# Statistics of the second image in layer 0: pieces of 512 pixels instead of 256, at six places of a period, loaded by ScalarE's queue

## The chip, the cores and the metric

The kernel runs on one core of a Trainium2 chip. The metric is the device time of one execution in microseconds; lower is better. Before the change it is 3701.71 us, the median of three runs (3700.44 to 3704.26). The engines are named as in the profile: PE is TensorE (PEld its weight loads), DVE is VectorE, ACT is ScalarE, POOL is GpSimd, SP is the engine that here only issues transfers.

## What is computed

Two images of 512 channels and 64 x 64 pixels go through two residual layers. Each layer first normalizes its input over groups of 16 channels and all pixels of an image. That is why an image's statistics must be complete before any of its pixels can be normalized.

```python
def _gn(v, G=32, eps=1e-5):
    g = v.reshape(B_, G, C_ // G, H_, W_)
    m = mean(g, axis=(2, 3, 4)); s = var(g, axis=(2, 3, 4))
    return ((g - m) / sqrt(s + eps)).reshape(v.shape)

x = x + _L0_conv_ref(_gn(x), ...)   # deformable convolution: project, depthwise 3x3,
                                    # layer norm over channels, gelu, offsets and masks,
                                    # bilinear samples summed over 9 points, output matrix
x = x + _L1_conv_ref(_gn(x), ...)   # attention over all pixels, matrix, batch norm, relu
```

The change touches only how `mean` and `var` of `_gn(x)` in layer 0 are gathered for the second image.

## The kernel before

**Tiling.** Channels lie on the 128 partitions in four blocks (`KB = 4`), pixels along the free axis in chunks of 512 (`CH`), which are eight rows of an image (`NCH = 8` chunks an image, 16 in all, `NSEQ`). All data are fp32.

**Stages of layer 0 for a chunk.** Each stage is a Python generator, and each `yield` ends a step:
- `project(i)` loads rows (`raw`, L737), normalizes them on ACT (`xn`, L748), multiplies them with `in_w` on PE (`pq`, L758), copies the result on ACT (`xj`, L764) and has SP store it to memory (`xt`, L766).
- `features(i)` is the depthwise convolution: one tap a channel block on ACT (L783), the other eight on DVE (`conv`, L788), then sums over channels: POOL adds the blocks (`tot`, L794 and L796), PE sums over partitions with a matrix of ones (`p_mean`, L801), DVE subtracts (L806), ACT squares (L809), POOL and PE sum again, ACT takes the root (L818), DVE the reciprocal (L820) and the product (L821), ACT the gelu (L825).
- `weights(i)` computes offsets and masks with PE (`po`, L842), adds a bias on DVE (`o`, L847) and makes sampling weights in a chain of pairs on DVE (`pk`, L885, and `aw`, L890); ACT copies them (`at`, L893), PE transposes them (`p_tr`, L901), ACT copies the result (`awT`, L902).
- `sample(i)` spreads the weights with PE (`pb`, L930) and ACT (`bt`, L935), multiplies with patches that SP has fetched from `xt` (`patch`, L914, eight transfers of 192 KB a fetch, two fetches a chunk) into `pa` (L949), which ACT copies to `dT` (L960); then the output matrix (`py`, L969), a residual add on DVE (L974) with statistics for layer 1 (L975), and SP stores the result (`wx`, L976).

**The period.** The 16 chunks are worked through in 16 periods. The function `period(y, v, m, w, f, g, p, more)` is an order written out by hand. It advances generators of several chunks by given numbers of steps: in period i, `p` is `project(i+3)`, `f` is `features(i+2)`, `w` is `weights(i+1)`, `v` the rest of `weights(i)` (its transposes), `m` is `sample(i)` and `y` the rest of `sample(i-1)`. Inside `tc.manual_schedule()` each engine executes its instructions in the order in which the program issues them, and waits for others by semaphores. A transfer is also issued in this order on the queue of the engine that is told to issue it, and holds that queue until what it waits for is done.

**The statistics.** `image_stats(n)` is one more generator. For image 0 it reads tiles that are in SBUF already, before the periods start. For image 1 it is the tail `later`, advanced by `more()`. Each step takes one piece of one channel block from memory (`xraw`, L711, three buffers, so loads run up to three pieces ahead) and has DVE make its statistics (`bn_stats`, L713). After the last piece of a block DVE combines them (`bn_aggr`, L715). Then `group_norm_steps` sums over the 16 channels of a group with two small matmuls (L602, L611), takes the root on ACT (L615) and the reciprocal on DVE (L618). Whatever is left of `later` is run in one go before period 5:

```python
for i in range(NSEQ):
    if i == NCH - 3:
        run(later)
    w, m, g = Chain(weights, i + 1), Chain(sample, i), Chain(features, i + 3)
    period(y, v, m, w, f, g, Chain(project, i + 3), lambda: next(later, None))
    y, v, f = m, w, g
```

Before the change a piece has 256 pixels, so image 1 has 4 x 16 = 64 of them; `period` calls `more()` at 13 places, eight in the loop over `taps` (two a round) and five in its second half; and SP issues the loads.

Of the kernel before, what the change touches and what calls it, by code (L numbers as in the profile page):

```python
# [9 lines left out]
F32 = mybir.dt.float32  # L10
# [7 lines left out]
P = 128  # L18
NB = 2
C = 512  # L20
KB = C // P
H = W = 64
S = H * W
# [7 lines left out]
CH = 512  # L31
NCH = S // CH
# [538 lines left out]
def window_path(ctx: ExitStack, tc: tile.TileContext, t_in: dict, out: bass.AP, far: bass.AP, sums: bass.AP):  # L571
    nc = tc.nc
    x_v = t_in["x"].rearrange("n (cb p) h w -> n p cb (h w)", p=P)
# [25 lines left out]
    def group_norm_steps(mv, k, small, psum, result):  # L599

        p1 = psum.tile([P, CH], F32, tag="mm", name="gn_p1")
        nc.tensor.matmul(p1[:, : 2 * k], gmat, mv.rearrange("p k s -> p (k s)"), start=True, stop=True)  # L602
        yield
        gm = small.tile([P, k, 2], F32, name=f"gn_gm{k}")
        nc.vector.tensor_copy(gm.rearrange("p k s -> p (k s)"), p1[:, : 2 * k])
        d = small.tile([P, k], F32, name=f"gn_d{k}")
        nc.vector.tensor_sub(d, mv[:, :, 0], gm[:, :, 0])
        nc.vector.tensor_mul(d, d, d)
        yield
        p2 = psum.tile([P, CH], F32, tag="mm", name="gn_p2")  # L610
        nc.tensor.matmul(p2[:, :k], gmat, d, start=True, stop=True)  # L611
        yield
        var = small.tile([P, k], F32, name=f"gn_var{k}")
        nc.vector.tensor_add(var, gm[:, :, 1], p2[:, :k])
        nc.scalar.activation(var, var, AF.Sqrt, bias=eps)  # L615
        yield
        sc = small.tile([P, k], F32, name=f"gn_sc{k}")
        nc.vector.reciprocal(sc, var)  # L618
        bi = small.tile([P, k], F32, name=f"gn_bi{k}")
        nc.vector.scalar_tensor_tensor(bi, gm[:, :, 0], -1.0, sc, ALU.mult, ALU.mult)  # L620
        result += [sc, bi]
# [8 lines left out]
    with ExitStack() as l0:  # L630
        wp = l0.enter_context(tc.tile_pool(name="w0w", bufs=1))
        io = l0.enter_context(tc.tile_pool(name="w0io", bufs=1))
        cv = l0.enter_context(tc.tile_pool(name="w0conv", bufs=1))
        sm = l0.enter_context(tc.tile_pool(name="w0small", bufs=1))
# [10 lines left out]
        img = [bt.rearrange("p g q d -> p (g q d)")[:, h * S : (h + 1) * S] for h in range(2)]  # L645
# [51 lines left out]
        def image_stats(n):  # L697

            mv = sm.tile([P, KB, 2], F32, name="gn_mv")
            size = CH if n == 0 else CH // 2  # L700
            pieces, ahead = deque((kb, h) for kb in range(KB) for h in range(S // size)), deque()
            for kb in range(KB):
                st = sm.tile([P, 16, 6], F32, name="gn_st")
                for h in range(S // size):
                    if n == 0:
                        t = img[kb][:, h * size : (h + 1) * size]
                    else:
                        while len(ahead) < 3 and pieces:
                            k2, h2 = pieces.popleft()
                            ahead.append(io.tile([P, size], F32, name="xraw", bufs=3))  # L710
                            nc.sync.dma_start(ahead[-1], x_v[n, :, k2, h2 * size : (h2 + 1) * size])  # L711
                        t = ahead.popleft()
                    nc.vector.bn_stats(st[:, h, :], t)  # L713
                    yield
                nc.vector.bn_aggr(mv[:, kb, :], st[:, : S // size].rearrange("p a b -> p (a b)"))  # L715
            yield
            result = []
            yield from group_norm_steps(mv, KB, sm, ps, result)
            sc, bi = result
            gn[n] = [sm.tile([P, KB], F32, name=f"gn_{k}{n}") for k in ("scale", "bias")]  # L720
            nc.vector.tensor_copy(gn[n][0], sc)
            nc.vector.tensor_copy(gn[n][1], bi)
# [275 lines left out]
        def period(y, v, m, w, f, g, p, more):  # L998

            p()
            y()
            v(4)
            f(4)
            y()
            for taps in (9, 7, 6, 6):
                m(2)
                w()  # L1010
                more()
                f(taps)
                w()
                more()
            w()
            m()
            w()
            m()
            f()
            y()  # L1020
            f()
            m()
            p()
            w(2)
            y(2)
            w()
            m()
            p()
            f()
            w(2)  # L1030
            p()
            y(2)
            f()
            y()
            m()
            p()
            more()
            for k, steps in enumerate((1, 2, 2, 2)):
                p()
                w(steps)  # L1040
                if k == 0:
                    f()
                p()
                more()
                if k < 3:
                    m()
                if k == 0:
                    f()
                if k == 2:
                    g()  # L1050
            w()
# [17 lines left out]
        def output_bias():  # L1069
# [8 lines left out]
            yield  # L1078

        run(image_stats(0), project(0), value_weights(), features(0), project(1))  # L1080
        v = Chain(weights, 0)
        v(23)
        run(features(1), project(2), output_bias())
        fetch(0, 0)
        fetch(0, 1)
        later, y, f = image_stats(1), Chain(sample, NSEQ), Chain(features, 2)
        with tc.manual_schedule():
# [7 lines that stand above are left out]
            y.rest()  # L1095
# [5 lines left out]
    with ExitStack() as l1, tc.manual_schedule():  # L1101
# [8 lines left out]
        with ExitStack() as at, ExitStack() as inner:  # L1110
# [69 lines left out]
            mv = bnp.tile([P, NB * KB, 2], F32, name="mv2")  # L1180
# [107 lines left out]
            for n in range(NB):  # L1288
# [9 lines left out]
                for i in range(NCH // 2):  # L1298
                    if 0 < i < 3 or n and i == 0:
                        k = i + 1 if i else 1  # L1300
# [26 lines left out]
                for qb in range(NCH):  # L1327
# [48 lines left out]
                    a = [acc[j].rearrange("p (cb q) -> p cb q", cb=2) for j in range(6)]  # L1376
# [156 lines left out]
```

## Time and profile before

The profiled execution took 3707.44 us; its span, from first to last instruction, is 3705.57 us.

| what | value |
|---|---|
| median of three runs | 3701.71 us |
| profiled execution, span | 3707.44 us, 3705.57 us |
| PE busy | 3417.9 us (92%) |
| DVE busy | 2345.8 us (63%) |
| ACT busy | 1304.1 us (35%) |
| mean granted TensorE clock | 0.968 |
| layer 0's periods 0 to 15 | about 172 to 1276 us |
| image 1's statistics, first to last | 175.1 to 533.0 us |

The page shows the span in 40 equal slices of 92.6 us. A digit is the busy share of the slice in tenths; in the row PEclk it is the granted clock in tenths.

```profile
PE   4689998999998799999999999999999999999990
DVE  5798989999996475545554554567455455545544
ACT  2476777787886321111111111221111111111114
PEclk9789999999999899999999999999999999999995
```

Layer 0 is the first third, where DVE, PE and ACT are all busy; layer 1 is the rest, where PE is. In the lists of instructions below, `out<-in` are names of tiles, then come partitions x elements and the count; brackets hold the idle time of the engine ahead of the instruction and what ended it. SPq and ACTq are the queues' own instructions, the issues of transfers.

### The profile page before, as it was taken

To read this page: it belongs to the slowest core of one execution; us is meant where nothing else is said; L and a number is where in the kernel's file an instruction comes from. 1 tells how busy PE (TensorE), PEld (TensorE's weight loads), DVE (VectorE), ACT (ScalarE), POOL (GpSimd) and SP (SyncE) were. 2 spreads that over 40 slices of the span, in tenths; PEclk is the share of its full clock that TensorE was granted. 3 is DMA by queue.
4 is the path that set the end of the run, shared out by engine and by line. 5 is a ranking of instruction groups with operands and counts; after the bars stand their busy time and mean duration, and the time that the engine had idled before them with its cause. 6 is when DMAs were issued, how large, how long until landed. Compare 5 with 4: busy or idle time off the path is not lost.

```text
span 3705.6 us, 39010 instructions
## 1 busy us (share of the span) xinstructions
PE 3417.9 (92%) x15151; PEld 2433.8 (66%) x15151; DVE 2345.8 (63%) x3575; ACT 1304.1 (35%) x1691; POOL 291.0 (8%) x190
## 2 busy tenths in 40 slices
PE   4689998999998799999999999999999999999990
PEld 1355555555555477777777777777777777777770
DVE  5798989999996475545554554567455455545544
ACT  2476777787886321111111111221111111111114
POOL 2112111212111030000000000022000000000000
PEclk9789999999999899999999999999999999999995
DMA  7233442342432444334334333444433333243349
GB/s 240 63 98 114 135 137 83 115 133 83 127 109 78 142 157 171 126 129 139 123 108 163 122 125 130 140 155 169 149 121 111 122 138 111 101 149 121 111 162 389
DMA packets 180181, 500.06 MB, mean 135 GB/s; under 512 B 22640, under 2 KB 64368, under 8 KB 170512
## 3 DMA queue, kind: packets, MB, share of 16 engines
q1 hardware_dynamic: 176496, 473.34, 37.5%
q10 hardware_dynamic: 3456, 24.12, 1.7%
q8 instruction: 121, 1.98, 0.2%
q14 instruction: 76, 0.62, 0.0%
q0 software_dynamic: 32, 0.00, 0.0%
HBM read 406.09 MB, written 91.29 MB: 134 GB/s over the span
## 4 chain that ended last, share of the span: by engine, by line
PE 75%; DVE 15%; DMA 4%; ACT 2%; SPq 1%; issue 1%; POOL 1%; ACTq 0%; DVEq 0%; POOLq 0%
PE acc L1364 41%; DVE conv L788 8%; PE pS L1211 7%; PE p L1402 7%; PE py L969 5%; PE pq L758 4%; PE pa L949 4%; PE pv L1251 3%; PE pk L1305 1%; PE p_mean L801 1%; DVE pk L885 1%; DVE aw L890 1%; DMA patch<-xt 1%; DMA out<-ct 1%; DVE o L847 1%
## 5 line engine op out<-in xcount | busy, mean ns | idle before, releaser
L1364 PE MATMUL acc<-e,v 128*128 128x256 f32 x3072 | 768.2, 386 | 0.0
L1215 ACT ACTIVATE e<-pS 128x1024 f32<-128x1024 f32 x256 | 262.0, 1024 | 1386.4 <-PE pS L1211 1313.0
L1364 PE MATMUL acc<-tt,v 128*128 128x256 f32 x3072 | 748.2, 380 | 0.5 <-DMA v<-wv 0.5
L1364 PEld LDWEIGHTS acc<-e,v 128*128 128x128 f32 x3072 | 566.5, 190 | 233.2 <-issue 165.3
L1364 PEld LDWEIGHTS acc<-tt,v 128*128 128x128 f32 x3072 | 582.4, 190 | 91.2 <-issue 10.6
L1218 DVE TENSOR_TENSOR t<-e 128x256 f32<-128x256 f32 x256 | 108.8, 425 | 761.1 <-ACT e L1215 761.1
L788 DVE SCALAR_TENSOR_TENSOR conv<-xn,L_conv_dw_w_sb,conv 128x504 f32<-128x504 f32 (+1 forms) x512 | 399.7, 795 | 48.5 <-ACT conv L783 36.5
L1228 DVE TENSOR_TENSOR tot<-tot,e 128x512 f32<-128x512 f32 x480 | 330.1, 688 | 8.3
L949 PEld LDWEIGHTS pa<-bt,patch 96*128 96x128 f32 x2048 | 251.8, 197 | 63.1 <-issue 39.4
L1211 PE MATMUL pS<-q,kq 64*128 64x512 f32 x1024 | 289.0, 641 | 0.0
L949 PE MATMUL pa<-bt,patch 96*128 96x128 f32 x2048 | 255.3, 281 | 9.3 <-ACT dT L960 5.8
L935 ACT COPY bt<-pb 96x1024 f32<-96x1024 f32 x124 | 234.2, 2001 | 58.9 <-PE pb L930 58.9
L758 PE MATMUL pq<-L_conv_in_w_sb,xn 128*128 128x512 f32 x512 | 236.3, 605 | 4.3 <-ACT xn L748 4.3
L969 PE MATMUL py<-dT,L_conv_out_w_sb 128*128 128x512 f32 x512 | 238.0, 610 | 0.0
L1402 PE MATMUL p<-t,v 128*128 128x256 f32 x1024 | 231.4, 382 | 1.7 <-DMA v<-wv 1.7
L1402 PEld LDWEIGHTS p<-t,v 128*128 128x128 f32 x1024 | 192.1, 190 | 48.5 <-issue 21.2
L960 ACT COPY dT<-pa 32x256 f32<-32x256 f32 x496 | 179.5, 362 | 89.8 <-PE pa L949 80.9
L842 PE MATMUL po<-om_w_pg,feat 128*128 128x432 f32 x512 | 203.4, 542 | 0.0
L969 PEld LDWEIGHTS py<-dT,L_conv_out_w_sb 128*128 128x128 f32 x512 | 99.3, 197 | 119.6 <-issue 115.5
L758 PEld LDWEIGHTS pq<-L_conv_in_w_sb,xn 128*128 128x128 f32 x512 | 94.1, 194 | 109.5 <-issue 93.0
L842 PEld LDWEIGHTS po<-om_w_pg,feat 128*128 128x128 f32 x512 | 93.0, 191 | 90.5 <-issue 89.4
L1211 PEld LDWEIGHTS pS<-q,kq 64*128 64x128 f32 x1024 | 77.1, 184 | 84.9 <-issue 84.9
(203 smaller groups left out, 3731.2 us busy)
## 6 DMA issues: line engine op xcount, KB each, us to landing
v<-wv SPq DMA_DIRECT2D x252, 768.0 KB
patch<-xt SPq DMA_DIRECT2D x256, 192.0 KB
v<-wv SPq DMA_DIRECT2D x256, 128.0 KB
wv<-v SPq DMA_DIRECT2D x32, 896.0 KB
xt<-xj SPq DMA_DIRECT2D x128, 128.0 KB
res<-in_x SPq DMA_DIRECT2D x64, 256.0 KB
wx<-res SPq DMA_DIRECT2D x64, 256.0 KB
xq<-wx SPq DMA_DIRECT2D x16, 1024.0 KB
```

Source lines behind the costliest of these rows:

```text
L758: nc.tensor.matmul(pq, xn[:, kb, 1 + 2 * t : 3 + 2 * t, :].rearrange("p r c -> p (r c)"), in_w[:, kb, :], start=(kb == 0), stop=(kb == KB ...
L788: nc.vector.scalar_tensor_tensor(dst, src, wt, dst, ALU.mult, ALU.add)
L842: nc.tensor.matmul(po[:, : 3 * GP], f[:, kb, t * P : (t + 1) * P], om_w[:, kb].rearrange("p a k g -> p (a k g)"), start=(kb == 0), stop=(k ...
L935: copy(bt[:SN].rearrange("s g q d -> s d (g q)")[:, d0 : d0 + 4, :], pb[:SN])
L949: nc.tensor.matmul(pa[:, p], xp[:SN, p, cb * P : (cb + 1) * P], bt[:SN, 4 * cb : 4 * cb + 4, PX * s + p, :], start=True, stop=True,)
L960: copy(dst, src)
L969: nc.tensor.matmul(py, out_w[:, kb, cb * P : (cb + 1) * P], dT[:, kb, :], start=(kb == 0), stop=(kb == KB - 1))
L1211: nc.tensor.matmul(pS[:, h, :], kq[r, 2 * (kp // 4) + h, c0 : c0 + P], qs[qb][r, :], start=True, stop=True)
L1215: nc.scalar.activation(e.rearrange("p a q -> p (a q)"), pS.rearrange("p h q -> p (h q)"), AF.Exp)
L1228: nc.vector.tensor_add(tots[qb], tots[qb], e2[:, h, :])
L1364: nc.tensor.matmul(acc[j][:, cb * HQ : (cb + 1) * HQ], v[:, j, cb * P : (cb + 1) * P], ops[j], start=(kp + cb == 0), stop=(kp + cb == NPAI ...
L1402: nc.tensor.matmul(p7[:, cb * HQ : (cb + 1) * HQ], v7[:, cb * P : (cb + 1) * P], t3, start=(k + cb == 0), stop=(k + cb == NPAIR + 2),)
```

## The change

A piece of image 1 now has 512 pixels, as one of image 0 has; there are 32. The buffers `xraw` double in size and stay three. The loads are issued by ACT's queue. `more()` is called at six places of a period instead of 13: after `v(4)`, after `f(4)`, in the rounds of 9 and 7 taps (after `f(taps)` and `w()`), in the second half after `y(2)` and before the step of `f` that holds the reciprocal, and once in the last loop (at `k == 2`).

```diff
             mv = sm.tile([P, KB, 2], F32, name="gn_mv")
-            size = CH if n == 0 else CH // 2
-            pieces, ahead = deque((kb, h) for kb in range(KB) for h in range(S // size)), deque()
+            pieces, ahead = deque((kb, h) for kb in range(KB) for h in range(NCH)), deque()
             for kb in range(KB):
-                st = sm.tile([P, 16, 6], F32, name="gn_st")
-                for h in range(S // size):
+                st = sm.tile([P, NCH, 6], F32, name="gn_st")
+                for h in range(NCH):
                     if n == 0:
-                        t = img[kb][:, h * size : (h + 1) * size]
+                        t = img[kb][:, h * CH : (h + 1) * CH]
                     else:
+
                         while len(ahead) < 3 and pieces:
                             k2, h2 = pieces.popleft()
-                            ahead.append(io.tile([P, size], F32, name="xraw", bufs=3))
-                            nc.sync.dma_start(ahead[-1], x_v[n, :, k2, h2 * size : (h2 + 1) * size])
+                            ahead.append(io.tile([P, CH], F32, name="xraw", bufs=3))
+                            nc.scalar.dma_start(ahead[-1], x_v[n, :, k2, h2 * CH : (h2 + 1) * CH])
                         t = ahead.popleft()
                     nc.vector.bn_stats(st[:, h, :], t)
                     yield
-                nc.vector.bn_aggr(mv[:, kb, :], st[:, : S // size].rearrange("p a b -> p (a b)"))
+                nc.vector.bn_aggr(mv[:, kb, :], st.rearrange("p a b -> p (a b)"))
```

```diff
             v(4)
+            more()
             f(4)
+            more()
             y()
             for taps in (9, 7, 6, 6):
                 m(2)
                 w()
-                more()
                 f(taps)
                 w()
-                more()
+                if taps in (7, 9):
+                    more()
...
             y(2)
+            more()
             f()
             y()
             m()
             p()
-            more()
             for k, steps in enumerate((1, 2, 2, 2)):
                 p()
                 w(steps)
                 if k == 0:
                     f()
                 p()
-                more()
+                if k == 2:
+                    more()
```

## The prediction

> **What bounds the kernel now.** I read the stretches first. I cut layer 0 where a period's first channel-mean matmul (`p_mean`, L801) starts, because that is where TensorE waits for VectorE. Columns: stretch, length, then busy time (instructions) of PE, PEld, DVE, ACT, POOL, then granted clock, DMA share, GB/s.
>
> ```profile
> core 0: us, PE busy (x) PEld busy (x) DVE busy (x) ACT busy (x) POOL busy (x), PEclk, DMA share, GB/s
> 203.20:275.00 71.80, 59.53 (x285) 37.73 (x285) 64.15 (x80) 53.84 (x74) 13.34 (x9) 0.88 0.38 119
> 275.00:351.70 76.70, 67.49 (x309) 39.27 (x309) 67.18 (x86) 53.76 (x72) 12.97 (x9) 0.95 0.40 122
> 351.70:426.00 74.30, 66.66 (x308) 39.06 (x308) 66.49 (x85) 53.69 (x73) 12.96 (x9) 0.96 0.40 126
> 426.00:500.00 74.00, 67.08 (x308) 39.21 (x308) 67.05 (x86) 53.77 (x73) 12.98 (x9) 0.96 0.39 125
> 500.00:575.30 75.30, 66.43 (x313) 39.52 (x313) 65.33 (x85) 55.07 (x75) 12.96 (x10) 0.95 0.33 103
> 575.30:646.00 70.70, 67.44 (x309) 39.47 (x309) 62.67 (x72) 53.56 (x72) 12.99 (x10) 0.96 0.35 108
> 646.00:713.70 67.70, 64.45 (x309) 38.35 (x309) 62.68 (x72) 53.80 (x72) 13.00 (x9) 1.00 0.36 113
> ```
>
> A period without statistics takes 67.7 us. One with them takes 74 to 77, although VectorE is busy only some 4.5 us longer. The rest shows in the timeline of TensorE (start, length, instruction, count, in brackets the idle time before it and what ended it), first with statistics, then without:
>
> ```profile
> 274.96 2.08 PE L801 MATMUL p_mean<-tot,ones_c 128*128 128x512 f32 x2 [5.87 <-POOL tot L796]
> 276.83 5.72 PE L969 MATMUL py<-dT,L_conv_out_w_sb 128*128 128x512 f32 x8
> ...
> 781.38 1.12 PE L801 MATMUL p_mean<-tot,ones_c 128*128 128x512 f32 x2 [1.25 <-POOL tot L796]
> 782.35 3.60 PE L969 MATMUL py<-dT,L_conv_out_w_sb 128*128 128x512 f32 x8
> ```
>
> TensorE idles 5.87 us instead of 1.25 (4.6 more), and then runs the next matmuls slowly: 2.08 for 1.12 and 5.72 for 3.60, another 3.1 us. 4.6 + 3.1 = 7.7, nearly all of the excess. Next, VectorE's timeline and the statistics' own instructions:
>
> ```profile
> 252.09 0.42 DVE L713 BATCH_NORM_STATS2 gn_st<-xraw 128x6 f32<-128x256 f32 x1
> 254.13 0.43 DVE L713 BATCH_NORM_STATS2 gn_st<-xraw 128x6 f32<-128x256 f32 x1 [1.62 <-DMA xraw<-in_x]
> ...
> 749.60 3.09 DVE L788 SCALAR_TENSOR_TENSOR conv<-xn,L_conv_dw_w_sb,conv 128x504 f32<-128x504 f32 x4 [1.82 <-ACT conv L783]
> 754.12 0.75 DVE L974 SCALAR_TENSOR_TENSOR res<-py,L_conv_out_b_sb,res 128x512 f32<-128x512 f32 x1 [1.42 <-PE py L969]
> 754.90 0.69 DVE L975 BATCH_NORM_STATS2 stats<-res 128x6 f32<-128x512 f32 x1
> ```
>
> ```profile
> L711 SPq DMA_DIRECT2D xraw<-in_x x64: 327/377/1118, 140.6 to 528.9; - x64
> L713 DVE BATCH_NORM_STATS2 gn_st<-xraw x64: 403/417/429, 175.1 to 533.0; 128x6 f32<-128x256 f32 x64
> ```
>
> So the loop of a period is: VectorE from the residual add L974 through 28 taps to the last `tot` (26 us), then TensorE from `p_mean` to the `py` that L974 waits for (40.4 us). What VectorE does between L974 and `tot` lengthens every period by its whole length. What it does elsewhere falls into its idle times: 1.82 us ahead of the four taps of `f(4)`, 1.42 ahead of L974. Today 8 of 13 pieces lie between L974 and `tot`.
>
> **What the Trainium skill says.** "TensorE: Matmul & The Clock Gate", Part 1 (The HAM clock gate), says that the array falls to half clock after about 3.4 us without work. The trace agrees at both ends: gaps of 4.4 to 7.3 us are followed by matmuls of 1061 ns, gaps of 1.2 to 1.3 by 592; between 1.3 and 4.4 no gap in this loop exists. "DMA: Bandwidth & Descriptors", Issuing engines are not separate DMA queues, says that issuing from two engines saves only sequencer time, since the same 16 DMA engines carry both. The trace shows nothing against it. So I expect no bandwidth from ScalarE's queue, only that loads no longer stand in line with SP's transfers.
>
> **The change, part by part.** I call the six places A to F: A after `v(4)`, B after `f(4)`, C and D in the rounds of 9 and 7 taps, E after `y(2)` before the reciprocal L820, F in the `pk`/`aw` chain. The order of the built program confirms them.
>
> *Cost of a piece.* 256 pixels: 417 ns, from start to next start 0.33. 512 pixels is not in these periods, but L975 is the same operation on 128x512: 0.69 long, 0.61 to the next start. VectorE in a period: 13 x 0.33 = 4.3 before, 6 x 0.61 = 3.7 after. The total hardly moves; the place does.
>
> *Between L974 and `tot`.* Removed: 8 x 0.33 = 2.6, the DMA wait (8.7 in all in five stalls, so 1.7 a period) and in two of the periods an aggregation (0.58). Added: C and D, 1.2, plus one aggregation (half as wide, 0.37) at C of period 1. The gap before `p_mean` becomes 1.25 + 1.2 = 2.5 (2.8 in period 1). That is under 3.4, so I take no half clock: between 0 and 3.1 us a period, I take 0.
>
> *A, B, E, F.* A (0.6) goes into the 1.82 of idle. So do F (0.6) and E, of which 0.5 remains since VectorE reaches L820 0.1 before its input: 1.7 in 1.82. B goes into the 1.42. Cost 0; if ScalarE's L783 slips, B's spare 0.8 takes it.
>
> *ScalarE's queue.* Six issues of some 0.4 us (SP's take 0.38) a period. C lies where ScalarE idles 0.42 waiting for `pb`, D where it idles 1.1, E and F where it idles 0.8 and 0.7 for `pa`; A and B together where it idles 1.21, ahead of the first `bt` (L935). Each load also waits. First, for the statistics that last used its buffer: already done in the steady order. Second, and this the diff does not show, for the transfer eight places earlier in program order, which shares its semaphore: the program's order makes B wait for the sixth of the eight patch transfers (L914), A for the fourth. By the trace's landings the sixth lands at 758.88 in the period at 749, one microsecond after the last `awT` copy (757.92). With F's 256 KB in the same window it may be 1 us later. Then the first `bt` starts at 760.3 instead of 759.13. Queued behind it are all `bt` copies, and TensorE's `pb`, `po`, `pa` wait for them. The second `po` would end at 768.3, VectorE wants it at 769.5; `pa` ends 1.2 later at 781.3, where TensorE now idles until 782.6. So 1.2 us costs nothing, and from about 2.4 on it costs its length. C's data, issued at A, land about 762 and are wanted at 762.9: I take 0, at worst 1.3 a period.
>
> *SP's queue.* 64 issues leave. Its patches and raws go out as in the later periods; no gain counted beyond the DMA wait.
>
> *Start, period 0.* SP now loads three pieces at 140.6, long before use. ScalarE's queue reaches its first load after the last `awT` copy (started at 176.1). With 0.4 for the issue and 2.4 to the landing (SP's 256 KB loads need 2.9 in all), piece A arrives at 178.9. VectorE stands there, since A comes before `f(4)`: A to 179.5, four taps to 182.6, B to 183.2, where before the nine taps began at 175.42. That is 7.8 late; then 7 x 0.33 fewer and 1.2 more: **+6.7 us** at `p_mean` of period 0. Less if the sequencer runs ahead, more if the landing is slow: 4 to 9.
>
> *End.* Six calls in five periods take 30 pieces; two remain and run in one go before period 5, with the group norm. VectorE waits there for TensorE and then ScalarE (the Sqrt with its table load ends at 544.4), so 2 x 0.6 + 0.4 is mostly hidden.
>
> *Sum*, as start of `p_mean`, before / after:
> - period 0: 203.2 / 209.9
> - 1: 275.0 / 209.9 + 39.9 to L974 + 27.3 + 1.2 + 0.4 = 278.7
> - 2: 351.7 / + 67.7 + 1.2 = 347.6
> - 3: 426.0 / 416.5
> - 4: 500.0 / 485.4
> - 5: 575.3 / + 75.2 less 2.1 (no slow `py` after the last gap) = 558.5
> - from there both equal: **-16.8 us**.
>
> Layer 1 follows unchanged. The profiled execution lasted 3707.4 (span 3705.6), so it would be 3690.6. The median shown, 3701.7, is 5.7 below it; taken off that, **3685 us**.
>
> **The rivals.**
> 1. *Half clock remains.* 2.5 us of idle might be enough, as the window that judges runs freely. For: at 1156.9, past the loop, 2.33 us of idle were followed within 2 us by transposes of 421 ns instead of 272. Against: the 3.4, and that stretch is sparse while this one is dense. Four gaps x 3.1 = 12.4 back: 3697, with C's data late as well 3700. Two of four: 3691.
> 2. *No stall at the start and C or D hidden.* For: ScalarE's sequencer may issue earlier than I think. 6.7 and up to 4 x 1.2 more: 3674.
> 3. *Slower: ScalarE is held at B by the patch transfers.* Loads now share the DMA engines with the patches instead of queueing behind them. If a patch fetch took twice as long, its sixth transfer would land 21 us after its start at 748.4 instead of 10.5, B would issue at 769.8, and `bt` be 10.7 late, 8.3 beyond the spare 2.4: 4 x 8.3 = 33, with the half clock kept 12.4: 3730. It outweighs the gain from a delay of about 5 us on. For: the wait is in the program. Against: 256 KB beside the fetch's 1.5 MB is a sixth, not a doubling.
> 4. *The change doesn't do what it says.* Excluded for places and sizes by the program's order; only the last two pieces stand elsewhere.
>
> **How the numbers follow.** Forecast 0.60 (its own range 3679 to 3691); rival 1 with all gaps 0.12, with some 0.10; rival 2 0.09; rival 3 0.09. Faster by over 0.2% (7.4 us, about what a measurement of this kernel can tell from no change): 0.60 + 0.09 + 0.10 = 0.79; within: 0.12; slower: 0.09. The range 3676 to 3700 holds all but rival 3 and the tail of rival 2.
>
> **What would show it.** The stretches between `p_mean` should be near 69 us from period 1 on with granted clock 1.00; gaps before `p_mean` 1.5 to 2.8; 32 statistics of about 0.69; no DMA wait at L713 but one of 5 to 6 us at 173 to 179. Wrong would be: matmuls of 1061 ns after those gaps, ScalarE idle ahead of L711 at B for over 2.4, or L974 later than 40.4 after `p_mean`.

## The result and the profile after

The changed kernel takes 3695.37 us, the median of 17 runs (3692.61 to 3697.63); the kernel before, on the same chip, 3701.95 us (17 runs, 3699.75 to 3705.36). The ratio is 0.9981, 95% interval 0.9974 to 0.9989: 6.6 us faster, where 16.8 were forecast. The profiled execution took 3696.76 us, its span 3694.6. The profiled execution of before, 3707.44, is slower than all 17 of its runs here, so the two traces lie 10.7 us apart and not 6.6; what follows therefore goes by single periods.

First the stretches of layer 0 after the change, again cut at the first `p_mean` of a period (stretch, length, busy time and instructions of PE, PEld, DVE, ACT, POOL, then clock, DMA share, GB/s):

```profile
core 0: us, PE busy (x) PEld busy (x) DVE busy (x) ACT busy (x) POOL busy (x), PEclk, DMA share, GB/s
209.10:278.70 69.60, 58.86 (x284) 37.12 (x284) 63.46 (x73) 53.85 (x73) 13.40 (x9) 0.92 0.39 121
278.70:351.50 72.80, 67.68 (x308) 39.31 (x308) 66.24 (x78) 53.66 (x73) 13.01 (x9) 0.96 0.40 127
351.50:422.50 71.00, 66.19 (x309) 38.94 (x309) 66.74 (x79) 53.90 (x73) 13.04 (x9) 0.98 0.41 130
422.50:492.60 70.10, 64.77 (x309) 38.22 (x309) 66.45 (x79) 53.77 (x73) 13.01 (x9) 1.00 0.41 130
492.60:568.20 75.60, 67.76 (x313) 39.49 (x313) 66.59 (x85) 55.07 (x76) 13.04 (x10) 0.95 0.34 107
568.20:637.40 69.20, 65.97 (x309) 38.97 (x309) 62.71 (x72) 53.63 (x72) 13.04 (x10) 0.98 0.36 110
```

The periods were to take 68.8, 68.9, 68.9, 68.9 and 73.1 us; they took 69.6, 72.8, 71.0, 70.1 and 75.6, which is 10.5 more. The clock, forecast at 1.00 from period 1 on, is 1.00 in one stretch only. TensorE's timeline at the four gaps (start, length, instruction, count, in brackets the idle time before it):

```profile
278.70 2.07 PE L801 MATMUL p_mean<-tot,ones_c 128*128 128x512 f32 x2 [3.17 <-POOL tot L796]
280.57 5.61 PE L969 MATMUL py<-dT,L_conv_out_w_sb 128*128 128x512 f32 x8
...
351.54 1.13 PE L801 MATMUL p_mean<-tot,ones_c 128*128 128x512 f32 x2 [2.93 <-POOL tot L796]
352.50 5.29 PE L969 MATMUL py<-dT,L_conv_out_w_sb 128*128 128x512 f32 x8
...
422.49 1.13 PE L801 MATMUL p_mean<-tot,ones_c 128*128 128x512 f32 x2 [2.77 <-POOL tot L796]
423.45 3.60 PE L969 MATMUL py<-dT,L_conv_out_w_sb 128*128 128x512 f32 x8
...
492.59 1.89 PE L801 MATMUL p_mean<-tot,ones_c 128*128 128x512 f32 x2 [3.19 <-POOL tot L796]
494.27 4.58 PE L969 MATMUL py<-dT,L_conv_out_w_sb 128*128 128x512 f32 x8
```

At these four places the gaps shrank from 5.0 to 7.3 us to about 3, as the new places should make them, but two things differ from the forecast. The gaps are 2.8 to 3.2 and not 2.5 to 2.8. And after three of the four the matmuls still run slowly: against 1.13 and 3.60 the two lines lose 2.95, 1.7, 0 and 1.7 us, 6.4 together.

VectorE's own lines show where the first difference comes from. First the statistics and their loads as groups (duration shortest/median/longest in ns, first and last start), then single ones from VectorE's timeline:

```profile
L711 ACTq DMA_DIRECT2D xraw<-in_x x32: 334/334/500, 174.5 to 526.1; - x32
L713 DVE BATCH_NORM_STATS2 gn_st<-xraw x32: 676/686/695, 177.8 to 529.9; 128x6 f32<-128x512 f32 x32
```

```profile
177.85 0.69 DVE L713 BATCH_NORM_STATS2 gn_st<-xraw 128x6 f32<-128x512 f32 x1 [6.15 <-DMA xraw<-in_x]
...
258.90 0.69 DVE L713 BATCH_NORM_STATS2 gn_st<-xraw 128x6 f32<-128x512 f32 x1 [0.39 <-DMA xraw<-in_x]
...
331.76 0.69 DVE L713 BATCH_NORM_STATS2 gn_st<-xraw 128x6 f32<-128x512 f32 x1 [0.94 <-DMA xraw<-in_x]
...
402.68 0.69 DVE L713 BATCH_NORM_STATS2 gn_st<-xraw 128x6 f32<-128x512 f32 x1 [0.24 <-DMA xraw<-in_x]
...
472.81 0.69 DVE L713 BATCH_NORM_STATS2 gn_st<-xraw 128x6 f32<-128x512 f32 x1 [1.12 <-DMA xraw<-in_x]
```

The first line is the stall at the start, as forecast. The other four are place C, which waits for its data in every period. In the third, ACT's queue issued the load at A at 325.13, and VectorE could go on at 331.76, 6.6 us later, where 0.4 for the issue and 2.4 to the landing had been counted.

The two kinds of loss are next taken apart: data that come late, and a clock that falls after gaps shorter than the forecast held for safe.

### The profile page after: what moved, and what is told of

Its sections match the earlier page's. It is cut to its first block, busy times and chain, and to the rows that moved or that the text cites. A ratio compares the mean times of both kernels' runs of the same rounds, so it can differ in the third digit from the quotient of the medians.

```text
span 3694.6 us, 38934 instructions
## 1 busy us (share of the span) xinstructions
PE 3418.5 (93%) x15151; PEld 2433.0 (66%) x15151; DVE 2349.0 (64%) x3543; ACT 1304.4 (35%) x1691; POOL 292.3 (8%) x190
## 4 chain that ended last, share of the span: by engine, by line
PE 76%; DVE 15%; DMA 4%; ACT 2%; issue 1%; POOL 1%; SPq 1%; ACTq 0%; DVEq 0%; POOLq 0%
PE acc L1367 42%; DVE conv L788 8%; PE pS L1214 7%; PE p L1405 6%; PE py L969 5%; PE pq L758 5%; PE pa L949 4%; PE pv L1254 3%; PE pk L1308 1%; PE p_mean L801 1%; DMA xraw<-in_x 1%; DMA out<-ct 1%; DVE o L847 1%; DVE pk L885 1%; DVE aw L890 1%
## 5 line engine op out<-in xcount | busy, mean ns | idle before, releaser
L935 ACT COPY bt<-pb 96x1024 f32<-96x1024 f32 x124 | 233.9, 2004 | 62.8 <-PE pb L930 51.6
```

Of the source, the lines that this page charges most:

```text
L935: copy(bt[:SN].rearrange("s g q d -> s d (g q)")[:, d0 : d0 + 4, :], pb[:SN])
```

## The experiments

All times are medians. The runs of the kernel before beside them had medians of 3703.98 (first four experiments), 3704.47 (the next four) and 3704.56 (two of the last, on another chip); each ratio is to those, and across these groups the ratios are what can be compared.

**Extra matmuls in the gap.** `mean_over_c` gets a number of matmuls on resident data, which the real sum then overwrites.

```diff
-            def mean_over_c(tot):
+            def mean_over_c(tot, fill=0):
                 p = ps.tile([P, CH], F32, tag="mm", name="p_mean")
+                for _ in range(fill):
+                    nc.tensor.matmul(p, ones, in_w[:, 0, :], start=True, stop=True)
                 nc.tensor.matmul(p, ones, tot, start=True, stop=True)
...
-            mu = mean_over_c(tot)
+            mu = mean_over_c(tot, {2: 4, 3: 2, 4: 2, 5: 2, 6: 2, 7: 4}.get(i, 0))
```

> The changed kernel with dummy matmuls (ones times a weight block, overwritten by the real product) ahead of the first channel mean: two for the chunks whose gap is about 3 us (periods 1 to 4), four for periods 0 and 5. Nothing else moves. Theory 1 (the gaps of 2.8 to 3.2 us still drop TensorE to half clock): the matmuls after these gaps run at 592 ns, the periods after them shrink by 3.0, 1.9, 0 and 1.9 us, that after period 5's gap by 1.5 to 2, layer 0 ends 7 to 9 us earlier than in the changed kernel, about 3687. Theory 2 (VectorE's total work sets the period, the slow matmuls are hidden behind it): the matmuls speed up but the distance between the means stays, 3695. If the fill is too long and delays the mean: later, with gaps gone.

Measured 3691.06 (7 runs), ratio 0.9971 (0.9960 to 0.9983). TensorE's timeline in period 1:

```profile
345.96 1.88 PE L802 MATMUL p_mean<-L_conv_in_w_sb,ones_c 128*128 128x512 f32 x4
348.97 1.12 PE L803 MATMUL p_mean<-tot,ones_c 128*128 128x512 f32 x2 [1.13 <-POOL tot L796]
349.93 3.60 PE L971 MATMUL py<-dT,L_conv_out_w_sb 128*128 128x512 f32 x8
```

The profile lists each of these matmuls twice, so x4 are the two extra ones. The sum comes no sooner, but the `py` after it are back at 3.60. The five periods took 68.9, 69.6, 69.8, 69.6 and 73.9 us: 7.2 of the 10.5 us are gone. Of these, 6.8 lie in TensorE's part of a period (from `p_mean` to L974), 6.4 of them in the slow lines; 0.4 lie in VectorE's part (from L974 to the next `p_mean`), since C's data came a little less late. In periods 0 and 5 gaps of 3.7 and 3.3 us remained in spite of four extra matmuls, and half clock followed.

The interval of the ratio overlaps that of the changed kernel, so the size rests on these periods. The traced execution as a whole shows nearly nothing of it: it took 3696.40 us, the changed kernel's 3696.76, and layer 1's first `pk` starts 0.8 us earlier where 7 to 9 were expected. Most was lost after the last `p_mean` of layer 0. From there to that `pk` the 12 traces of whole kernels need either 160 to 161 us (the changed kernel 160.7) or 164 to 165 (this run 164.4, the kernel before 164.8). TensorE's work has gaps there, and the four long cases have half clock for 27.3 us in one piece, the eight short ones for 17.1 at most.

**C and D moved to the chain.** Pieces at k = 1, 2 and 3 of the last loop, none between the taps.

```diff
-                if taps in (7, 9):
-                    more()
...
-                if k == 2:
+                if k > 0:
                     more()
```

> The changed kernel with pieces C and D taken out of the rounds of taps and put into the last loop, so that three pieces lie in the pk/aw chain (k = 1, 2, 3). Theory 1 (only what stands between the residual add and tot lengthens a period; elsewhere it fills idle time): gaps before the mean 1.3 to 1.7 us, matmuls after them at 592 ns, periods 1 to 4 near 68 us instead of 69.6, 72.8, 71.0, 70.1, layer 0 about 13 us earlier than in the changed kernel, 3682. Theory 2 (VectorE's total work sets the period): the same six pieces cost the same, 3695. Theory 3 (ScalarE's queue holds the period): unchanged or worse, since more loads stand just before L783.

Measured 3709.26 (17 runs), ratio 1.0014 (1.0007 to 1.0021), slower than before. VectorE waits for `xraw` 31.5 us in seven stalls. First ACT's timeline, then VectorE's:

```profile
320.61 0.34 ACTq L711 DMA_DIRECT2D xraw<-in_x  x1
```

```profile
326.86 0.69 DVE L713 BATCH_NORM_STATS2 gn_st<-xraw 128x6 f32<-128x512 f32 x1 [4.18 <-DMA xraw<-in_x]
```

A load is issued two places ahead of its use. With three pieces in a row, and A and B soon after, the load for B goes out at k = 3, at 320.61, and is wanted some 2 us later. The waits cost more than C and D had cost. So the place of a piece isn't free to choose: it also sets when a later load starts.

**First three loads on SP's queue.**

```diff
-                            nc.scalar.dma_start(ahead[-1], x_v[n, :, k2, h2 * CH : (h2 + 1) * CH])
+                            (nc.sync if (k2, h2) < (0, 3) else nc.scalar).dma_start(ahead[-1], x_v[n, :, k2, h2 * CH : (h2 + 1) * CH])
```

> The changed kernel with the first three loads on SP's queue, where they are issued long before use. Theory 1: the stall of 6.15 us ahead of the first statistics goes, the first mean of period 0 comes at 202.5 to 203.5 instead of 209.1, the rest as in the changed kernel, 3689. Rival (the stall only moves the gap that period 0 has anyway, behind ScalarE's waits for VectorE at B and D): less than 2 us, 3694.

Measured 3689.42 (5 runs), ratio 0.9960 (0.9946 to 0.9973). The first `p_mean` of period 0 starts at 202.1 instead of 209.1, and the wait for `xraw` falls from 9.3 us to 1.6. So the stall at the start cost 7.0 us in the trace; in the times it is 6 us by the medians, 8 by the ratios. The gaps were 2.83, 3.17, 2.52 and 2.42, and the `py` slow after all but the one of 3.17: the length of a gap alone doesn't decide.

**All loads on SP's queue**, sizes and places as changed.

```diff
-                            nc.scalar.dma_start(ahead[-1], x_v[n, :, k2, h2 * CH : (h2 + 1) * CH])
+                            nc.sync.dma_start(ahead[-1], x_v[n, :, k2, h2 * CH : (h2 + 1) * CH])
```

> The changed kernel with all loads back on SP's queue: sizes and places alone. If the queue brings the gain: the loads wait behind patches and stores as before the change, each stalls VectorE at C by 1 to 2 us, and gaps go back to 4 to 5 us with half clock in each period, 3700 or above, less the first stall of 6 us (which goes, as the loads can be early). If the places bring it: 3689, the changed kernel less the first stall.

Measured 3700.65 (21 runs), ratio 0.9990 (0.9984 to 0.9997). Waits for `xraw` are 10.8 us in five stalls, the gaps 4.5 to 4.95, all followed by half clock. Against the run with early loads, which differs only in the queue of the later loads, that is 11 us slower.

**C alone moved**, to k = 1.

```diff
-                if taps in (7, 9):
+                if taps == 7:
                     more()
...
-                if k == 2:
+                if k in (1, 2):
                     more()
```

> The changed kernel, but place C (the round of nine taps) is gone and a piece is taken at k == 1 of the last loop, ahead of the one at k == 2. Theory (a gap ahead of p_mean costs its length and, from somewhere near 2.4 us, half clock after it; C also takes late data): the gap falls to about 1.25 + 0.6 = 1.9 us in periods 1 to 4, the matmuls after it take 592 ns, no wait for xraw is left at the taps, periods 1 to 4 take about 68.5 us, and the whole about 12 us less than the changed kernel (some 3683). Rival 1 (the lead of three buffers is too short once two pieces lie close together): DVE waits for xraw at A or B for 2 us or more a period and the time is at that of the changed kernel or above it. Rival 2 (the place C costs nothing, the rest of the gap has another cause): gaps stay at 2.7 to 3.2 and the time within 3 us of the changed kernel.

Measured 3687.98 (5 runs), ratio 0.9957 (0.9944 to 0.9971): 7.4 us less than the changed kernel, where some 12 were expected. The only wait for `xraw` left is the one at the start (5.9). Periods 1 to 4 took 70.0, 68.3, 68.3 and 73.9. TensorE's timeline at the end of period 1, where the gap had been 2.93:

```profile
349.04 1.13 PE L801 MATMUL p_mean<-tot,ones_c 128*128 128x512 f32 x2 [1.68 <-POOL tot L796]
350.00 3.60 PE L969 MATMUL py<-dT,L_conv_out_w_sb 128*128 128x512 f32 x8
```

Three of the four gaps (1.68, 1.74, 1.87) are followed by full clock; the one of 2.21 at 279.0, with the aggregation in it, is not.

**C moved and the first loads on SP's queue**, by the edits of the two runs named together.

> The kernel of the run before with the first three loads on SP's queue. Theory: the two gains are of different periods and add up: the 7 us stall of period 0 goes, and the gaps are as in the run before, so about 3676. Rival (the lead is too short): the 7 us alone, at the level of the kernel with early loads or above it (3689 or more).

Measured 3684.29 (5 runs, 3678.21 to 3685.19), ratio 0.9941 (0.9928 to 0.9955). In the trace the gains add up: layer 1's first `pk` starts at 1255.9 instead of 1264.0. In the medians only 3.7 of the 7 show, and the expected 3676 was not reached. The traced execution took 3679.68; the two executions below 3680 had a mean granted clock of 0.972 and 0.973, the three at 3684 and 3685 had 0.971.

**Extra matmuls in the kernel before**, by the same edit to `mean_over_c`, with `{2: 3, 3: 4, 4: 4, 5: 4, 6: 3, 7: 4}`.

> The kernel before, with three or four extra matmuls on resident data ahead of p_mean in the chunks whose gap is long (2: 3, 3 to 6: 4 or 3, 7: 4); their results are overwritten by the real sum. Theory (half clock was worth 3.1 us a period before the change, and the rest of the loss is the length of VectorE's work): matmuls of 592 ns after p_mean in most of these periods and 8 to 15 us less than before, so 3688 to 3695; p_mean still comes late by 4.6 us. Rival (half clock is no cost of its own because VectorE sets the time of the period): within 3 us of before.

Measured 3704.33 (13 runs, 3698.32 to 3708.17), ratio 0.9999 (0.9991 to 1.0007). This missed: the time is the one that the rival expected. The extra matmuls run as soon as TensorE is free, and between them and the late sum gaps of 2.2 to 4.2 remained, followed by half clock in three of five places; the waits for `xraw` were 10.5 us. In the trace, which is of the fastest of the 13 executions, the five periods are 4.0 us shorter than before, in the medians nothing is left. So the run doesn't tell what the clock alone was worth before the change.

**Queue alone**: 256 pixels and 13 places, loads on ScalarE's queue.

```diff
-                            nc.sync.dma_start(ahead[-1], x_v[n, :, k2, h2 * size : (h2 + 1) * size])
+                            nc.scalar.dma_start(ahead[-1], x_v[n, :, k2, h2 * size : (h2 + 1) * size])
```

> The kernel before, with its pieces of 256 pixels at 13 places, and the loads alone moved to ScalarE's queue. Theory (queue move takes out the waits for data at the taps, but ScalarE's queue is late once at the start and carries 64 issues of 0.33 us): the wait for xraw falls from 8.7 us in five to some 5 at the start and little later; start 4 to 7 us late; layer 0 ends within 6 us of before, so the queue alone brings no clear gain. Rival 1 (the queue carries most of the gain): 6 us or more faster than before. Rival 2 (64 issues hold up ScalarE's copies): 5 us or more slower.

Measured 3708.30 (21 runs), ratio 1.0012 (1.0005 to 1.0019): 3.8 us slower. First `p_mean` at 207.6, 4.4 later than before, as expected. The waits for `xraw` at the taps, though, were to go with the queue and did not: of 13.0 us in all, 5.3 are at the start and 7.7 in four later stalls. Queue alone costs 3.8, sizes and places alone bring 3.3, together they bring 6.6: the parts don't add, the queue helps only with the new sizes and places.

**Statistics from resident data.** The loads stay; VectorE no longer waits for them.

```diff
-                        t = ahead.popleft()
+                        ahead.popleft()
+                        t = in_w[:, 0, :]
...
-            nc.vector.tensor_copy(gn[n][0], sc)
-            nc.vector.tensor_copy(gn[n][1], bi)
+            nc.vector.tensor_copy(gn[n][0], gn[0][0] if n else sc)
+            nc.vector.tensor_copy(gn[n][1], gn[0][1] if n else bi)
```

> The changed kernel, whose loads are all issued as before while the statistics of image 1 read resident weights (in_w, 128x512) in place of the piece, so that VectorE never waits for a load; image 1 is then normalized with image 0's scale and bias. This leaves out the second image's true statistics. Theory (two terms of the gap were missed: late data for C, some 0.5 us a period, and half clock after gaps that the forecast held for safe): no wait before L713, first p_mean at 203, gaps of 2.5 to 2.8 in periods 1 to 4, and still matmuls of 1061 ns after at least one and perhaps all four of them; 9 us less than the changed kernel, some 3686. Rival 1 (late data alone lifted the gaps over an edge near 2.8): no matmul of 1061 ns after these gaps, some 3680. Rival 2 (the gap doesn't come from the two pieces and their data): gaps of 2.9 to 3.2 remain.

Measured 3686.84 (5 runs), ratio 0.9952 (0.9938 to 0.9965). The gaps are now 2.78, 2.44, 2.38 and 1.90, the forecast's own 2.5 to 2.8 or less. Two of them in TensorE's timeline:

```profile
342.79 1.15 PE L802 MATMUL p_mean<-tot,ones_c 128*128 128x512 f32 x2 [2.44 <-POOL tot L797]
343.76 5.29 PE L970 MATMUL py<-dT,L_conv_out_w_sb 128*128 128x512 f32 x8
...
413.40 1.12 PE L802 MATMUL p_mean<-tot,ones_c 128*128 128x512 f32 x2 [2.38 <-POOL tot L797]
414.36 3.60 PE L970 MATMUL py<-dT,L_conv_out_w_sb 128*128 128x512 f32 x8
```

One of two nearly equal gaps is followed by half clock, the other not; of the four, three are, even that of 1.90. VectorE's part of periods 0 to 3, from L974 to the next `p_mean`, takes 28.9, 28.5, 28.5 and 28.5 us, exactly what the forecast has. The five periods exceed the forecast by 6.1 us, of which these slow lines are 5.0. So with data always in time the forecast still fails, and mainly by the clock; this run's rival 1 falls.

**Moved, early, and filled** where half clock was left: chunks `{2: 3, 3: 2, 7: 4}`.

> C moved to k == 1 and the first three loads on SP's queue as in the run before, and extra matmuls on resident data ahead of p_mean in the chunks whose gap was still followed by half clock (chunk 2: three, 3: two, 7: four). Theory (each of these gaps costs about 2 us by the clock alone): 592 ns after them, 3 to 5 us less than without the extra matmuls, some 3680. Rival (these gaps stand where TensorE doesn't set the time of the period): within 1.5 us of it, 3684.

Measured 3678.71 (5 runs, 3677.28 to 3680.18), ratio 0.9932 (0.9918 to 0.9945). It is the fastest version, 26 us under the kernel before beside it. Against the run without extra matmuls that is 3.3 us less by the ratios, as expected, though the intervals overlap. In the trace full clock follows at chunks 2 and 3; at chunk 7 a gap of 3.3 us and half clock remain.

**The gap by itself.** A small kernel: bursts of matmuls, then two operations of VectorE that the next burst waits for. Its main part (`...` marks lines left out):

```python
SIZES = (64, 256, 512, 768, 1024, 1280, 1536, 1792, 2048, 2304, 2560, 2816, 3072, 3328, 3584, 4096)
REPS = 10
...
        for k in range(REPS * len(SIZES)):
            size = SIZES[k * 7 % len(SIZES)]
            for j in range(36 + k * 5 % 13):
                p = ps.tile([P, 512], F32, tag="p", name="p")
                nc.tensor.matmul(p, w, r if j else s[:, :512], start=True, stop=True)
            nc.vector.tensor_scalar(s[:, 0:16], p[:, 0:16], 0.5, None, ALU.mult)
            nc.vector.tensor_scalar(s[:, :size], s[:, :size], 0.999, None, ALU.mult)
```

> Measures the disputed cost by itself and computes nothing of the reference: 160 bursts of 36 to 48 matmuls 128x512 fp32, with an idle stretch of TensorE between them that VectorE sets (two operations, the second on 64 to 4096 elements a partition, in a mixed order), so gaps from about 1 to some 5 us, ten of each length. Theory (a window that runs by itself judges TensorE's work): no half clock after short gaps, then a band of lengths in which some gaps of the same length are followed by 1061 ns and others not, with a share that grows with the length, and all of them above; the band holds 2.2 to 3.2 us. Rival (an edge in the gap's own length, as the forecast took it): one length below which none and above which all are followed by half clock.

The second sweep has longer operations, and the tile `s` is made wide enough for them:

```diff
-SIZES = (64, 256, 512, 768, 1024, 1280, 1536, 1792, 2048, 2304, 2560, 2816, 3072, 3328, 3584, 4096)
+SIZES = tuple(3072 + 384 * k for k in range(16))
```

> The gap sweep again, with the second operation of VectorE on 3072 to 8832 elements a partition, so gaps of some 2.2 to 5.2 us; it computes nothing of the reference. Theory (a window of fixed length, run through without regard to the gap, has to fall into the idle time far enough): the share of gaps followed by 1061 ns goes on rising from about half at 2.2 to 2.7 us and reaches all of them at about twice the length at which the first appear (1.8), so near 3.6 us. Rival (an edge in the gap's own length, blurred a little): all gaps from about 2.9 us on are followed by half clock.

Counted from both traces, 318 gaps; slow means that matmuls of about 1061 ns follow:

```
gap us     0.6-1.8  1.9   2.0   2.2    2.3   2.4   2.6-2.7  2.8   3.0   3.2   3.4   3.6   3.8-5.2
slow/all   0/99     1/10  2/10  11/20  5/10  8/20  11/20    7/10  6/10  8/10  9/10  9/10  79/79
```

Both expectations of a band hold, but it is wider than the first expected (2.2 to 3.2 us): half clock first appears at 1.9, and every gap has it only from 3.8. Half clock after a gap lengthened the burst by 1.7 us on average in the first sweep and by 2.0 in the second, by 3.1 at most. Why equal gaps differ is seen in stretches of 3.41 us: in each of the 14 traces the granted clock changes only at multiples of 3.413 us from one another (to 0.011 us). Two gaps of 2.15 us in the first sweep, one slow, one not, cut on that grid (stretch, length, busy time and instructions of PE, PEld, DVE, POOL, then granted clock):

```profile
core 0: us, PE busy (x) PEld busy (x) DVE busy (x) POOL busy (x), PEclk, DMA share, GB/s
2636.48:2639.89 3.41, 1.26 (x3) 0.49 (x3) 1.93 (x2) 0.00 (x0) 1.00 0.00 0
2639.89:2643.30 3.41, 3.41 (x5) 1.33 (x4) 0.00 (x0) 0.00 (x0) 0.50 0.00 0
...
4469.43:4472.85 3.42, 2.19 (x6) 0.64 (x4) 1.16 (x2) 0.00 (x0) 1.00 0.00 0
4472.85:4476.26 3.41, 2.48 (x6) 1.25 (x7) 0.78 (x1) 0.00 (x0) 1.00 0.00 0
4476.26:4479.67 3.41, 3.41 (x9) 1.52 (x8) 0.00 (x0) 0.00 (x0) 1.00 0.00 0
```

In the first case the whole gap lies in one stretch; TensorE is busy 1.26 of 3.41 there, and the next stretch runs at 0.50. In the second the gap is cut by the grid, both halves are busy 2.19 and 2.48, and the clock stays. The same cut in the changed kernel, at two of its gaps (columns as in the first table):

```profile
core 0: us, PE busy (x) PEld busy (x) DVE busy (x) ACT busy (x) POOL busy (x), PEclk, DMA share, GB/s
349.46:352.87 3.41, 1.33 (x3) 0.68 (x4) 3.27 (x5) 2.20 (x6) 1.27 (x1) 1.00 0.00 0
352.87:356.29 3.42, 3.42 (x5) 1.35 (x4) 3.42 (x3) 1.29 (x4) 0.00 (x0) 0.50 0.00 0
...
417.72:421.14 3.42, 2.00 (x18) 1.81 (x17) 3.28 (x6) 0.00 (x0) 0.00 (x0) 1.00 0.00 0
421.14:424.55 3.41, 2.06 (x5) 1.06 (x6) 3.27 (x4) 2.89 (x8) 1.26 (x1) 1.00 0.01 2
424.55:427.96 3.41, 3.41 (x16) 2.02 (x15) 3.41 (x3) 1.21 (x4) 0.00 (x0) 1.00 0.00 0
```

The gap of 2.93 fell into one stretch (busy 1.33, half clock next), the one of 2.77 into two (2.00 and 2.06, full clock). A grid that runs on through the program decides, by the idle time that falls into one stretch. It is not tied to the program: its place against the start of the span differs from run to run, from 0.3 to 3.2 us in the 14 traces.

## Why the prediction was half right

**The bound and the places: right.** The loop from L974 through the taps to `tot` and through TensorE to `py` set the periods. Moving pieces out of it shortened the gaps, and moving one more (C) shortened them again, to 1.7 to 1.9 us, with periods of 68.3.

**The start: right.** +6.7 was forecast at the first `p_mean` (209.9); it came at 209.1, +5.9, by a stall of 6.15 at A. Taken out, it gave back 7.0 in the trace.

**"That is under 3.4, so I take no half clock: between 0 and 3.1 us a period, I take 0": the step that failed.** The Trainium skill, "TensorE: Matmul & The Clock Gate", Part 1, says that the window is some 3.4 us and runs freely; the traces agree, with 3.413. But the page has a whole window idle before the clock falls, and here the measurement decides: about half a window is enough. In the 14 traces, a stretch of the grid at full clock in which TensorE was busy for less than 1.4 us was followed by half clock in all 304 cases, one with more than 1.7 in 12 of 15,219; between the two there are both (13 of 62). Hence a gap can cost from about 1.9 us on, and surely costs from about 3.8, since at best the grid cuts it into two halves of 1.9. At the forecast's own 2.5 us some half of all gaps are followed by half clock, and the changed kernel's were, three of four: 6.4 us by the slow lines, 6.8 by what the extra matmuls took back in TensorE's part. Rival 1 had named it, with 1156.9 in the trace of before as its evidence, and set its price: two of four gaps 3691, all four 3697, all with late data 3700. With three of four and late data the result, 3695.4, lies between these. Rival 1's 3.1 us a gap is the dearest in the trace of before: the lines after its four gaps lose 3.1, 2.3, 2.6 and 1.5.

**"C's data: I take 0, at worst 1.3 a period": a term mis-sized.** C waited 0.39, 0.94, 0.24 and 1.12 us, 2.7 together. VectorE's part of periods 0 to 3 took 29.2, 29.5, 28.8 and 29.7 us, 2.8 more than the forecast's 28.9 and three times 28.5, and in the run on resident data this excess is gone. The loads issued at A needed 5.9 to 6.8 us from issue to landing, not 2.8. The landing records of the trace (each transfer's semaphore) show where such times occur. Loads issued during a patch fetch landed after 4.3 to 6.8 us, four issued just behind one after 5.0 to 5.4, all others after 2.7 to 4.1. The trace of before has the same difference: its 128 KB loads took 5.4 to 6.7 us in the midst of a fetch and 2.1 to 2.4 in most other places. Of the sixteen shares in which the load at 325.13 landed, eight were there after 3.5 us and the rest after 5.5 to 6.6, and a patch transfer lands in eight shares only. So the load probably has to share half of the DMA engines with the fetch; no run took the fetch away, so this is not shown.

**The account.** 10.5 us more than forecast over five periods. The clock took 6.4: TensorE's part of periods 1, 2 and 4 was 43.4, 42.1 and 48.2 us, against 40.4, 40.4 and 46.5 with extra matmuls in the gap. Late data took 2.8. In the last period the forecast erred by another 0.7, for the most part because it took off 2.1 for slow lines that in the trace of before lost only 1.5 (2.08 and 4.12 for 1.12 and 3.60). The remaining 0.5 lie in TensorE's part of period 0 (40.4 for 39.9), and their cause is open. The first `p_mean` was 0.8 earlier than forecast, so 9.7 of the forecast's 16.8 were lost by period 5, which leaves 7.1 in the traces; 6.6 was measured. That the two are so close is partly luck, since the time after the last `p_mean` of layer 0 differs by another 4 us between the two traces (164.8 and 160.7).

**Rivals 2 to 4.** Rival 2 (a free start) did not happen by itself. Rival 3, ScalarE held at B by the patches: in the trace of after its `bt` (L935) waited for `patch` once, an idle time of 1.82 us where before it was 1.21, so 0.6 late and inside the spare of 2.4. Rival 4 was excluded, rightly.

## What to carry to other kernels

Price an idle gap of TensorE by where it can fall on the clock's grid: up to 1.8 us it cost its length, above it up to 3 us more in a share of cases. Moving one piece (0.6 us of VectorE's work, and its wait for data) out of the gap was worth as much as the whole change (7.4 us). Read a load's time to landing where it will run: beside the patch fetch it was about twice the one elsewhere. When a consumer of prefetched data is moved, also move through the loads that its use triggers: with three buffers, three uses close together left the later load without time. A load moved to another queue is timed by that queue's place in the program; its first use needs an earlier issue of its own.

## What was not expected of the hardware

TensorE's clock changed only on a grid of 3.413 us in every trace, whatever the gaps; half clock came in whole stretches of it, so 1.7 us is the cost of one busy stretch at half clock, and 2.95 was measured where it lasted two. It needed no idle stretch: 1.33 us of work in 3.41 were not enough to keep the clock, 2.00 were. The way back asks for more: a stretch at half clock with less than 2.75 us of work was never followed by full clock (0 of 628 in the 14 traces), one with 3.0 or more nearly always was (296 of 302). So two gaps of equal length (2.15 us) ended differently by where the grid cut them.

The grid lies differently in every traced run, so the same kernel should keep the clock in one execution and lose it in the next. Each kernel was traced only once, but the mean granted clock of its executions does vary: of the 13 of the kernel before with extra matmuls, the four fastest (3698.3 to 3700.8 us) had 0.972 or 0.973, the other nine (3701.0 to 3708.2) 0.969 to 0.971.
